# A graph network's first 112 nodes leave the count matrix and get their neighbours by row gathers

## The chip, the cores and the metric

The kernel runs on one core of one Trainium2 chip. The metric is the device time of one execution, in microseconds (us). The kernel before was run three times: 517.18, 517.28 and 517.34 us, median 517.28.

## The reference, cut to what matters

A graph has 2500 nodes with 256 numbers each and 80000 edges, sorted by target node. The input is normalized and clipped at zero, then three edge convolutions follow, and at the end a product with a wide matrix is added to the input:

```python
def _edge_conv(x, src, dst, W, b):
    m = concatenate([x[dst], x[src] - x[dst]], axis=-1) @ W + b      # W is 512 x 256
    s = segment_sum(m, dst, num_segments=2500)
    cnt = segment_sum(ones, dst, num_segments=2500)
    return s / maximum(cnt, 1.0)[:, None]

h = maximum(layernorm(x), 0.0); xs = [h]
for W, b in ((W0, b0), (W1, b1), (W2, b2)):
    h = relu(_edge_conv(h, src, dst, W, b)); xs.append(h)
return x + concatenate(xs, axis=-1) @ Wf + bf
```

A node's sum is its edge count times `h @ (W_top - W_bottom)`, plus the sum of the rows `z = h @ W_bottom` of the sources of its edges, plus the count times `b`.

## The kernel before, in words

**The count matrix.** The sum over sources is a dense matrix product. `A[s, n]` says how many edges run from node s to node n. The 2500 source nodes lie in NT = 20 tiles of 128, one tile after the other on the partitions. The target nodes are columns. Six neighbouring targets make a window (W = 6), 417 windows in all (NW). The windows are cut into five groups (GWS): four of 84 windows (504 columns) and one of 81 (486 columns). A group's part of A is a tile `a` of 128 x 20 x 512 floats (`new_a`, two of them in memory), of which 504 columns are used.

**Building A.** For each window the edges are fetched by an indirect transfer from GpSimd (`get_edges`, up to 256 edges for each of 128 windows). `compare` (lines 755 to 769) lets VectorE write one-hot matrices `one_m` and `one_n` for four windows at a time. `counts` multiplies them on TensorE into PSUM, two matmuls for each window. `take_counts` (line 782) lets ScalarE copy the result into `a`. `finish` (line 800) lets GpSimd put the edge counts themselves into a spare row of `a` (PAD = 96 of the last tile), so that `b` comes in by the same product, and stores the tile in HBM (`a_dram`), from where layers 2 and 3 load it (`load_a`).

**Aggregating.** `z` is held as two float32r halves, `zh` (rounded) and `zl` (the rest). `layer` (line 817) runs for each group 20 tiles x 2 column halves x 2 parts = 80 float32r matmuls of the group's width into `pa` (line 832), and then 4 float32 matmuls (8 records in the profile) that add `h @ (W_top - W_bottom)` times the count (line 836). ScalarE writes the clipped result into `hT` (line 839). `hT` holds h transposed: nodes in the columns.

**The order of the work.** Before line 847 comes a head: loading, normalizing, the first products, and the building of group 0. Its order is written out by hand as a string of short names (lines 864 to 873); the recorder `InOrder` (line 270) keeps program order on each engine, and what is recorded by it shows as line 280 in the profile. In layer 1 (`l = 0`, lines 900 to 928) the groups run from 0 to 4, and the building of the next group is spread between the matmuls of the present one. In layers 2 and 3 (`l = 1, 2`, lines 931 to 958) first `nodes_split` (line 708) computes z for all 20 tiles (2 matmuls each, line 711), which ScalarE and VectorE split into `zh` and `zl`. Then for each group come the `final` products of its tiles (line 734, with VectorE adding into `acc` at line 736) and `layer`. Layer 2 runs the groups backwards. In layer 2 `add_x` (line 724) loads each tile of x from GpSimd's queue and adds it and `bf`, on GpSimd. The last 20 `final` products and the stores of the output end the kernel.

The `bank` tiles of PSUM, which `nodes_split` and `final` share, are four in number here. In SP's queue stand the stores and loads of `a`, the weights and the output. In GpSimd's queue stand the indirect transfers and the loads of x.

Of the kernel before, what the change touches and what calls it, by code (L numbers as in the profile page):

```python
# [311 lines left out]
def by_windows(ctx: ExitStack, tc: tile.TileContext, x, src, dst, Ws, bs, Wf, bf, out, missing):  # L312
# [15 lines left out]
    CAP = CH * P  # L328
    NW = (N + W - 1) // W
    NV = NW * W  # L330
    WG = (NW + P - 1) // P
    NB = NT * W
    BW = 4
# [4 lines left out]
    while sum(GWS) < NW:  # L338
        GWS.append(min(84, NW - sum(GWS)))
    G = max(GWS) * W  # L340
    GS = 512
    NG = len(GWS)
# [6 lines left out]
    assert NP <= 4096 and HR <= 512  # L349
    assert E == P * R and NV <= NP and BW * NB <= 512 and G <= 512 and CAP <= 256  # L350
    assert E + P < 2 ** 24 and NV - (NT - 1) * P <= PAD < P and D == DC * P

# [35 lines left out]

    const.tile([P, 24], F32, name="between")
    a_dram = [dram.tile([P, NT, G], F32, name=f"a_dram{g}") for g in range(NG)]  # L390

# [42 lines left out]

    lim_i = pp.tile([P, WG], I32, name="lim_i")
    POOLo.iota(lim_i, pattern=[[P * W, WG]], base=0, channel_multiplier=W)
    limr_i = pp.tile([P, WG * P], I32, name="limr_i")
    POOLo.iota(limr_i, pattern=[[W, WG * P]], base=0, channel_multiplier=0)
    row_i = pp.tile([P, MORE], I32, name="row_i")
# [14 lines left out]
    DVE.memset(ones_b, 1.0)  # L454
    DVE.memset(cnt[:, NV:], 0.0)
    POOL.tensor_copy(ident_b, ident)
    warm = pp.tile([P, 1], F32, name="warm")
    ACTo.activation(warm, ones, AF.Sqrt)
# [95 lines left out]
    def key_parts(i):  # L554
# [4 lines left out]
        parts[i] = [lo_i]  # L559

    def key_low(i):
        km = pw.tile([P, CAP], F32, name="km")
        ACTo.copy(km, parts[i][0])
        parts[i][0] = km

    def key_high(i):

        hi_i = edges[i][0]
        DVEo.tensor_scalar(hi_i, hi_i, ~(P - 1), 4, op0=OP.bitwise_and, op1=OP.logical_shift_right)
        kn = pw.tile([P, CAP], F32, name="kn")  # L570
        DVEo.scalar_tensor_tensor(kn, away[:, i, :], float(W), hi_i, op0=OP.min, op1=OP.add)
        parts[i].append(kn)
# [15 lines left out]
    def degrees(i):  # L588

        for q in range(W + 2):  # L590
            junk = hot.tile([P, CAP], BF16, name="junk2")
            ACTo.activation(junk, away[:, i, :], AF.Relu, bias=nc_[:, q:q + 1], accum_out=gsum[:, i, q:q + 1])
            yield
        DVEo.scalar_tensor_tensor(deg[:, i, :], gsum[:, i, 1:W + 1], -2.0, gsum[:, i, 0:W], op0=OP.mult, op1=OP.add)
        DVEo.tensor_add(deg[:, i, :], deg[:, i, :], gsum[:, i, 2:W + 2])
        DVEo.tensor_copy(deg_b[:, i, :], deg[:, i, :])
        yield
        yield
        yield
        yield  # L600
        for w0 in range(0, min(P, NW - i * P), P // 2):
            n = min(P // 2, NW - i * P - w0)
            pc = bank()
            for c in range(W):
                PEo.matmul(pc[:, :n * W].rearrange("p (w c) -> p w c", c=W)[:, :, c],
                          deg_b[:, i, c:c + 1].to_broadcast([P, P]), ident_b[:, w0:w0 + n], start=True, stop=True)
            ACTo.copy(cnt[:, (i * P + w0) * W:(i * P + w0 + n) * W], pc[:, :n * W])
            yield

    def shares():  # L610
        cnt_n = bank()
        for t in range(NT):
            PEo.matmul(cnt_n[:, t:t + 1], cnt[0:1, t * P:(t + 1) * P], ones_b, start=True, stop=True)
        found = hot.tile([P, 1], F32, name="found")
        DVEo.reduce_sum(found, deg.rearrange("p i c -> p (i c)"), axis=mybir.AxisListType.X)
        pf = bank()
# [90 lines left out]

    def nodes_split(l, t):
        pz = bank()
        for c in range(DC):  # L710
            PE.matmul(pz[:, :D], hT[:, c, t * P:(t + 1) * P], ws[l][1][:, c, :],  # L711
                      start=(c == 0), stop=(c == DC - 1))
        sc = share[:, t:t + 1]
        if t == NT - 1:
            zf = hot.tile([P, D], F32, name="zf")
            DVE.scalar_tensor_tensor(zf, pz[:, :D], sc, brow[:, l % 2, :], op0=OP.mult, op1=OP.add)
            ACT.copy(zh[:, t, :], zf)
            DVE.tensor_sub(zl[:, t, :], zf, zh[:, t, :].bitcast(F32))
        else:
            ACT.activation(zh[:, t, :], pz[:, :D], AF.Copy, scale=sc)  # L720
            DVE.scalar_tensor_tensor(zl[:, t, :], pz[:, :D], sc, zh[:, t, :].bitcast(F32),  # L721
                                     op0=OP.mult, op1=OP.subtract)

    def add_x(t):
        n = P if t < NT - 1 else LAST
        xb = hot.tile([P, D], F32, name="zf")
        POOL.dma_start(xb[:n], x[t * P:t * P + n, :])
        POOL.tensor_add(xb[:n], xb[:n], bf_sb[:n])
        POOL.tensor_add(acc[:n, t, :], acc[:n, t, :], xb[:n])

    def final(l, t):
        po = bank()
        for c in range(DC):
            PE.matmul(po[:, :D], hT[:, c, t * P:(t + 1) * P], wfs[l][:, c, :],  # L734
                      start=(c == 0), stop=(c == DC - 1))
        DVE.scalar_tensor_tensor(acc[:, t, :], po[:, :D], share[:, t:t + 1], acc[:, t, :], op0=OP.mult, op1=OP.add)  # L736
        if l == L:
            n = P if t < NT - 1 else LAST
            SP.dma_start(out[t * P:t * P + n, :], acc[:n, t, :])


    def group_of(g):
        return sum(GWS[:g]) * W, GWS[g] * W

# [55 lines left out]
    def finish(g, a):  # L800
        c0, n = group_of(g)
        POOLo.tensor_copy(a[PAD:PAD + 1, NT - 1, :n], cnt[PAD:PAD + 1, c0:c0 + n])
        SP.dma_start(a_dram[g][:, :, :n], a[:, :, :n].bitcast(F32))
# [8 lines left out]
    def by_count(g):  # L812
        c0, n = group_of(g)
        for o in range(DC):
            DVEo.tensor_mul(hT[:, o, c0:c0 + n], hT[:, o, c0:c0 + n], cnt[:, c0:c0 + n])

    def layer(l, g, a, own, PE=PE, ACT=ACT):
# [29 lines left out]
    groups = [(0, 1), (1, 2), (2, 4), (4, 6), (6, 8), (8, Q)]  # L847
    a = new_a(0)
    acts = {
        "lim": limits, "first": find_first, "next": find_next, "pick": find_rows,  # L850
        "dstr": lambda: ACTo.copy(dst_r[:, MORE:], dst_i),
        "pk": lambda i: pick_half(i // 10, i % 10), "sg": lambda i: count_half(i // 10, i % 10),
        "se": lambda i: search(*((0, 1), (1, WG))[i]), "ge": get_edges,
        "ka": key_parts, "km": key_low, "kb": key_high, "kt": key_turn,
        "k1": lambda i: key_copy(i, 0), "k2": lambda i: key_copy(i, 1),
# [3 lines left out]
        "Z": lambda q: product(q, ws[0][1]), "V": lambda q: with_b(), "H": split_high, "L": split_low,  # L859
        "F": lambda q: product(q, wfs[0]), "G": first_final,  # L860
        "B": compare, "C": counts, "E": lambda b: take_counts(b, a),
        "warm": keep_warm,
# [6 lines left out]
        k11 N8 L6 B4 E2 L5 C3 B5 C4 T8 E3 E4 C5 V9 R8 E5 ge3 ka2 H9 sc2 Z7 H7 F8 G7 B6 N3 N2 ka3 km2 T2 R2 km3  # L869
        kb2 C6 T3 kb3 B7 L7 kt2 Z2 B8 B9 L9 E6 C7 k22 k12 kt3 H2 N4 E7 B10 k13 k23 Z8 L2 C8 T4 C9 E8 C10 H8 E9  # L870
        F9 B11 B12 C11 G8 E10 C12 R4 E12 E11 B13 F5 B14 C13 R3 B15 C14 E13 E14 L8 B16 Z3 G9 B17 C15 C16 H3 E15
        G5 B18 F3 C17 E16 C18 F4 E17 B19 C19 Z4 L3 G3 B20 E18 C20 B21 F2 E19 B22 E20 H4 L4 G4 B23 B24 G2 ws
    """
# [23 lines left out]
    held = None  # L897
    LATE = [NT] * 4
    extra = chain(degrees(0), finish(0, a), later_loads(), degrees(1))
    for g in range(NG):  # L900
# [12 lines left out]
        for u, _ in enumerate(layer(0, g, a, own, PEo, ACTo)):  # L913
# [7 lines left out]
            if u == NT - 1 and g + 1 < NG:  # L921
                run(extra)
                by_count(g + 1)
        run(extra)
        if g + 1 < NG:
            run(finish(g + 1, a1))
            held, a = a, a1
        extra = chain(degrees(g + 2) if g + 2 < WG else ())
    DVEo.tensor_sub(ws[1][0], ws[1][0], ws[1][1])
    tiles = {NG - 1: a, NG - 2: held}  # L930
    for l in range(1, L):
# [3 lines left out]

        last = touched(groups[0])
        for t in [t for t in range(NT) if t not in last] + last:
            nodes_split(l, t)
        if l + 1 < L:
            load_b(l + 1)  # L940
            load_wb(l + 1)
            load_wt(l + 1)
        finished = set()
        for j, g in enumerate(groups):
            for t in touched(g):
                if t not in finished:
                    finished.add(t)
                    final(l, t)
                    if l == 1:
                        add_x(t)  # L950
            if j == NG - 1:
                load_wf(l + 1)
            run(layer(l, g, tiles[g], LATE))
            if j == 1 and l + 1 < L:
                DVEo.tensor_sub(ws[l + 1][0], ws[l + 1][0], ws[l + 1][1])
            if j + 2 < NG:
                del tiles[g]
                tiles[groups[j + 2]] = load_a(groups[j + 2])

    for t in [*range(NT - 3), NT - 1, NT - 3, NT - 2]:  # L960
# [39 lines left out]
```

## Time and profile before

| | us |
|---|---|
| median of three runs | 517.28 |
| the profiled execution, whole | 517.24 |
| its span, first to last instruction | 515.4 |
| head, until the matmuls of group 0 begin | 62.33 |
| layer 1, groups 0 to 3 with the building of the next | 127.85 |
| layer 1, group 4 | 20.34 |
| `nodes_split` of layer 2, then its five groups | 17.27, then 124.25 |
| `nodes_split` of layer 3, then its five groups | 17.26, then 124.01 |
| last products and output | 22.09 |

The stages are cut where the chain of work that ended last passes from one to the next. The profile lists engines as PE (TensorE's matmuls), PEld (its weight loads, which run beside matmuls), DVE (VectorE), ACT (ScalarE), POOL (GpSimd) and SP (SyncE, which here issues transfers). A busy time is the time in which at least one instruction of the engine runs; matmuls are pipelined, so the duration of a record is longer than the distance from its start to that of the next, and only the distance counts in a sum. The chain follows the work back from the last instruction, at each step to what released it.

### The profile page before, as it was taken

Reading aid. Unit: us, or ns where it says so; the run is one execution under the profiler, and the core shown is the slowest. Engines: PE = TensorE matmul, PEld = TensorE weight load, DVE = VectorE, ACT = ScalarE, POOL = GpSimd, SP = SyncE. Lnnn points to the kernel's source line nnn. Section 1 sums busy time; section 2 is a strip of 40 time slices with the busy share of each in tenths; the row PEclk is TensorE's granted clock in tenths of the full one; section 3 lists DMA queues with packets and bytes.
Section 4 is the critical chain, followed back from the end, with each engine's and each line's share of the span. In section 5 each row is a group of like instructions: output and inputs, shape, how many; then the busy total and the mean of one; then the engine's idle time right before and its main releaser. Section 6 shows DMA issues by size and latency. Waiting matters only on the chain.

```text
span 515.4 us, 6981 instructions
## 1 busy us (share of the span) xinstructions
PE 508.1 (99%) x2864; PEld 407.2 (79%) x2864; DVE 213.5 (41%) x455; ACT 134.1 (26%) x307; POOL 68.5 (13%) x103
## 2 busy tenths in 40 slices
PE   8999999999999999999999999999999999999996
PEld 4898888778778788788787878787887878787875
DVE  7989998889888840360101010103501010101033
ACT  5776666644534320330000000004300000000000
POOL 2680000000000000017241424200000000000000
PEclk9999999999999999999999999999999999999999
DMA  9110008950906428011576665100005565730023
GB/s 277 50 43 0 1 2 325 336 215 15 378 11 232 171 80 318 22 31 48 180 261 207 236 229 214 32 1 1 1 0 197 205 219 183 252 136 20 1 84 121
DMA packets 38111, 68.74 MB, mean 133 GB/s; under 512 B 1201, under 2 KB 37065, under 8 KB 38071
## 3 DMA queue, kind: packets, MB, share of 16 engines
q1 hardware_dynamic: 35798, 63.49, 34.8%
q0 software_dynamic: 1344, 3.61, 2.3%
q10 hardware_dynamic: 928, 1.11, 0.7%
q8 instruction: 24, 0.39, 0.3%
q14 instruction: 17, 0.13, 0.1%
HBM read 40.03 MB, written 28.18 MB: 132 GB/s over the span
## 4 chain that ended last, share of the span: by engine, by line
PE 90%; DVE 4%; DMA 3%; POOL 2%; issue 1%; SPq 0%; DVEq 0%
PE pa L832 35%; PE pa L280 21%; PE bank L734 10%; PE bank L280 8%; PE bank L711 7%; PE pa L836 7%; PE pz L280 2%; DMA acc<-in_x_dram 2%; POOL acc L280 1%; DVE one_m L280 1%; DVE st L280 1%; DMA es<-in_src_dram,start_i 1%; POOL ed L280 1%; DVE one_n L280 1%; POOL es L280 0%
## 5 line engine op out<-in xcount | busy, mean ns | idle before, releaser
L832 PE MATMUL pa<-a,zh 128*128 128x504 f32 (+1 forms) x400 | 156.4, 391 | 0.0
L832 PE MATMUL pa<-a,zl 128*128 128x504 f32 (+1 forms) x400 | 154.5, 386 | 0.0
L736 DVE SCALAR_TENSOR_TENSOR acc<-bank,share,acc 128x256 f32<-128x256 f32 x60 | 29.0, 484 | 213.6 <-PE bank L734 213.5
L832 PEld LDWEIGHTS pa<-a,zh 128*128 128x128 f32 x400 | 75.2, 188 | 14.9
L832 PEld LDWEIGHTS pa<-a,zl 128*128 128x128 f32 x400 | 75.1, 188 | 14.8
L280 PE MATMUL pa<-a,zh 128*128 128x504 f32 (+1 forms) x200 | 84.0, 420 | 0.0
L280 DVE TENSOR_TENSOR one_m<-iota_m,key_m 128x1024 bf16<-128x1024 bf16 (+1 forms) x105 | 72.1, 687 | 15.2 <-PE bank L280 15.1
L280 PE MATMUL pa<-a,zl 128*128 128x504 f32 (+1 forms) x200 | 77.7, 389 | 0.0
L839 ACT ACTIVATE hT<-pa 128x1008 f32<-128x1008 f32 (+1 forms) x10 | 10.1, 1005 | 238.8 <-PE pa L836 238.8
L280 ACT CAST a<-bank 128x480 fp32r<-128x480 f32 (+1 forms) x105 | 52.9, 565 | 68.5 <-PE bank L280 65.9
L280 DVE TENSOR_TENSOR one_n<-iota_n,key_n 128x960 bf16<-128x960 bf16 (+1 forms) x105 | 69.7, 664 | 0.0
L734 PE MATMUL bank<-wf,hT 128*128 128x256 f32 x240 | 53.6, 379 | 0.0
L734 PEld LDWEIGHTS bank<-wf,hT 128*128 128x128 f32 x240 | 45.6, 190 | 9.8 <-issue 4.1
L280 PEld LDWEIGHTS <-one_m 128*128 128x128 bf16 x834 | 45.5, 98 | 9.8 <-issue 7.0
L280 PE MATMUL bank<-one_n,one_m 128*128 128x120 bf16 x834 | 51.4, 217 | 0.3
L280 PEld LDWEIGHTS pa<-a,zh 128*128 128x128 f32 x200 | 37.8, 189 | 10.3 <-issue 2.6
L280 PEld LDWEIGHTS pa<-a,zl 128*128 128x128 f32 x200 | 37.7, 189 | 8.9 <-issue 2.6
L721 DVE SCALAR_TENSOR_TENSOR zl<-bank,share,zh 128x256 fp32r<-128x256 f32 x38 | 18.4, 484 | 56.0 <-ACT zh L720 55.9
L836 PE MATMUL pa<-hT,wt 128*128 128x504 f32 (+1 forms) x80 | 35.2, 582 | 0.0
L711 PE MATMUL bank<-wb,hT 128*128 128x256 f32 x160 | 34.9, 379 | 0.0
L711 PEld LDWEIGHTS bank<-wb,hT 128*128 128x128 f32 x160 | 30.4, 190 | 4.9 <-issue 0.9
L836 PEld LDWEIGHTS pa<-hT,wt 128*128 128x128 f32 x80 | 15.1, 189 | 14.5 <-issue 13.8
(113 smaller groups left out, 333.2 us busy)
## 6 DMA issues: line engine op xcount, KB each, us to landing
a<-a_dram SPq DMA_DIRECT2D x5, 5040.0 KB, 17.3
a_dram<-a SPq DMA_DIRECT2D x4, 5040.0 KB, 17.2
a_dram<-a SPq DMA_DIRECT2D x1, 4860.0 KB, 17.1
a<-a_dram SPq DMA_DIRECT2D x1, 4860.0 KB, 15.1
zf<-in_x_dram POOLq DMA_DIRECT2D x19, 128.0 KB, 4.2
out_dram<-acc SPq DMA_DIRECT2D x19, 128.0 KB, 1.7
wf<-in_L_gnn_Wf_dram SPq DMA_DIRECT2D x4, 256.0 KB, 9.0
acc<-in_x_dram SPq DMA_DIRECT2D x1, 896.0 KB, 10.1
```

What stands on the lines that cost most here:

```text
L280: return self.tc.keep_in_program_order(call(*args, **kwargs))
L711: PE.matmul(pz[:, :D], hT[:, c, t * P:(t + 1) * P], ws[l][1][:, c, :], start=(c == 0), stop=(c == DC - 1))
L721: DVE.scalar_tensor_tensor(zl[:, t, :], pz[:, :D], sc, zh[:, t, :].bitcast(F32), op0=OP.mult, op1=OP.subtract)
L734: PE.matmul(po[:, :D], hT[:, c, t * P:(t + 1) * P], wfs[l][:, c, :], start=(c == 0), stop=(c == DC - 1))
L736: DVE.scalar_tensor_tensor(acc[:, t, :], po[:, :D], share[:, t:t + 1], acc[:, t, :], op0=OP.mult, op1=OP.add)
L832: PE.matmul(pa[:, o, :n], z[:, i, o * P:(o + 1) * P], a[:, i, :n], start=(i == 0 and z is zh), stop=(z is zl and last[o] == (kind, i, o)))
L836: PE.matmul(pa[:, o, :n], ws[l][0][:, c, o * P:(o + 1) * P], hT[:, c, c0:c0 + n], start=False, stop=(last[o] == (kind, i, o)))
L839: ACT.activation(hT[:, :, c0:c0 + n], pa[:, :, :n], AF.Relu)
```

## The change

The first FEW = 112 nodes are no longer columns of A. NW becomes 398 windows (2388 nodes), and the groups become four of 80 windows (480 columns) and one of 78 (468 columns); GS, the row length of `a`, becomes 480, so that four of the five tiles are stored and loaded as one run for each partition. `group_of` starts at column 112.

For the 112 nodes, `few_edges` (act `ix`) writes the numbers of up to EDGES = 60 sources of each into `who`, on the partitions 14 to 125 of the last batch of edges. Where there is no such edge it writes the last row, 2559, which is zero. z is kept in HBM as a table of rows, `z_dram[l]`:

- In layer 1, `keep_nodes` (acts `X` and `Y`) stores `zh` from SP and adds `zl` onto it from GpSimd, in five pieces. `gather(0)` then issues 60 indirect transfers from GpSimd, each of one row for every partition, that add into eight tiles `sums`; `add_sums(8)` lets VectorE add the eight.
- In layers 2 and 3 `nodes_split` writes z in float32 first (`zf`, on ScalarE, in memory of `one_m`, `sums` and `one_n`); SP stores it tile by tile, and VectorE makes `zh` and `zl` out of it with two instructions. `gather_pairs` issues 60 gathers, two for each of 30 pairs, into the four buffers of `one_m`, and VectorE adds each pair into `sums`, four pairs behind.
- `layer_few` runs at the end of each layer: for each column half 2 float32 matmuls with the weights, 2 float32r matmuls with `cnt_few` (for the count times `b`), and 1 float32 matmul with `only`, which places the gathered sums; all are 112 columns wide. ScalarE clips the result into the first 112 columns of `hT`.

`add_x` becomes `add_rest`: VectorE adds `bf` to a group's tiles at once, and GpSimd issues a transfer that adds x. The row of counts in `finish` is copied by ScalarE in place of GpSimd. The order string loses the windows 20 (C, E) and 24 (B) and gains `ix`, five `X` and five `Y`.

```diff
-    NW = (N + W - 1) // W
+    FEW = 112
+    EDGES = 60
+    SUMS = 8
+    PAIRS = 4
+    NW = (N - FEW) // W
...
-        GWS.append(min(84, NW - sum(GWS)))
+        GWS.append(min(80, NW - sum(GWS)))
     G = max(GWS) * W
-    GS = 512
+    GS = 480
...
+    def few_edges():
+
+        es, ed = edges[WG - 1]
+        own = pp.tile([P, EDGES], I32, name="own")
+        POOLo.tensor_scalar(who, es[:, :EDGES], -NONE, None, op0=OP.add)
+        POOLo.tensor_scalar(own, away[:, WG - 1, :EDGES], 0.0, None, op0=OP.is_equal)
+        POOLo.tensor_tensor(who, who, own, op=OP.mult)
+        POOLo.tensor_scalar(who, who, NONE, None, op0=OP.add)
...
-            ACT.activation(zh[:, t, :], pz[:, :D], AF.Copy, scale=sc)
-            DVE.scalar_tensor_tensor(zl[:, t, :], pz[:, :D], sc, zh[:, t, :].bitcast(F32),
-                                     op0=OP.mult, op1=OP.subtract)
...
+            ACT.activation(zf, pz[:, :D], AF.Copy, scale=sc)
+        SPo.dma_start(z_dram[l][t * P:(t + 1) * P, :], zf)
+        DVEo.tensor_copy(zh[:, t, :], zf)
+        DVEo.tensor_sub(zl[:, t, :], zf, zh[:, t, :].bitcast(F32))
...
+    def gather(l):
+
+        for e in range(EDGES):
+            POOLo.indirect_dma_start(
+                out=sums[:, e % SUMS, :], out_offset=None, in_=z_dram[l][:, :],
+                in_offset=bass.IndirectOffsetOnAxis(ap=who[:, e:e + 1], axis=0),
+                **({"compute_op": OP.add} if e >= SUMS else {}))
...
+    def gather_pairs(l):
+
+        got = []
+        for k in range(EDGES // 2 + PAIRS):
+            if k >= PAIRS:
+                if k == PAIRS + 1:
+                    DVEo.tensor_add(sums[:, :2, :], got[0], got[1])
+                elif k > PAIRS:
+                    DVEo.tensor_add(sums[:, :2, :], sums[:, :2, :], got[k - PAIRS])
+            if k < EDGES // 2:
+                two = room()
+                got.append(two)
+                for i in range(2):
+                    POOLo.indirect_dma_start(
+                        out=two[:, i, :], out_offset=None, in_=z_dram[l][:, :],
+                        in_offset=bass.IndirectOffsetOnAxis(ap=who[:, 2 * k + i:2 * k + i + 1], axis=0))
+            if k >= PAIRS - 1:
+                yield
+
+    def layer_few(l):
+        pa = ps_agg.tile([P, DC, 512], F32, name="pa")
+        for o in range(DC):
+            for c in range(DC):
+                PEo.matmul(pa[:, o, :FEW], ws[l][0][:, c, o * P:(o + 1) * P], hT[:, c, :FEW],
+                           start=(c == 0), stop=False)
+            for z in (zh, zl):
+                PEo.matmul(pa[:, o, :FEW], z[:, NT - 1, o * P:(o + 1) * P], cnt_few, start=False, stop=False)
+            PEo.matmul(pa[:, o, :FEW], sums[:, 0, o * P:(o + 1) * P], only, start=False, stop=True)
+        ACTo.activation(hT[:, :, :FEW], pa[:, :, :FEW], AF.Relu)
...
+    gather(0)
     extra = chain(degrees(0), finish(0, a), later_loads(), degrees(1))
...
+    add_sums(SUMS)
+    layer_few(0)
     DVEo.tensor_sub(ws[1][0], ws[1][0], ws[1][1])
...
+        last = [t for t in touched(groups[0]) if t]
+        for t, zf in zip([t for t in range(1, NT) if t not in last] + last + [0], rooms(l)):
+            nodes_split(l, t, zf)
+        few = gather_pairs(l)
+        next(few)
...
-            run(layer(l, g, tiles[g], LATE))
+            for u, _ in enumerate(layer(l, g, tiles[g], LATE)):
+                if 4 <= u < NT and u % 2 == 0:
+                    next(few, None)
+                if rest and u in (1, NT):
+                    next(rest, None)
...
+        run(few)
+        add_sums(2)
+        layer_few(l)
```

In the order in which the changed kernel is built, TensorE has 1200 float32r matmuls of aggregation as before (960 of 480 columns, 240 of 468), 796 count matmuls in place of 834, the same number of line 711 and 734 products, and 16 more records in each layer for `layer_few`, which stands behind the last group of its layer. In layers 2 and 3 tile 0, whose columns `layer_few` writes last, is the last that `nodes_split` treats. VectorE's 29 additions of pairs stand in its queue between the `final` additions of one group and those of the next: 7, 8, 8 and 6 of them.

## The prediction

> **What bounds the kernel now.** I read the busy times and the slices first, then the chain of waits by line and in order of time, then the stages, then the rows of the transfers that the change multiplies.
>
> ```profile
> PE 508.1 (99%) x2864; PEld 407.2 (79%) x2864; DVE 213.5 (41%) x455; ACT 134.1 (26%) x307; POOL 68.5 (13%) x103
> ...
> POOL 2680000000000000017241424200000000000000
> ...
> PE 90%; DVE 4%; DMA 3%; POOL 2%; issue 1%; SPq 0%; DVEq 0%
> PE pa L832 35%; PE pa L280 21%; PE bank L734 10%; PE bank L280 8%; PE bank L711 7%; PE pa L836 7%; PE pz L280 2%; DMA acc<-in_x_dram 2%; POOL acc L280 1%; DVE one_m L280 1%; DVE st L280 1%; DMA es<-in_src_dram,start_i 1%; POOL ed L280 1%; DVE one_n L280 1%; POOL es L280 0%
> ```
>
> A busy TensorE alone proves little; the chain does: 90% of it is TensorE, 56% the aggregation alone (L832 35%, L280 21%). POOL, which gets the new work, is empty for most of the span. The chain in order of time gives prices free of overlap:
>
> ```profile
> 78.93 1.28 PE bank L280 x24
> ...
> 210.52 17.27 PE bank L711 x80
> ...
> 256.41 18.15 PE pa L832 x80
> 274.56 3.38 PE pa L836 x8
> ...
> 472.70 17.34 PE pa L832 x80
> 490.05 3.26 PE pa L836 x8
> ```
>
> A 504-column matmul costs 18.15/80 = 226.9 ns, a 486-column one 17.34/80 = 216.8; a float32 record 422 and 407; a count matmul 1.28/24 = 53. In layer 1 VectorE might share the bound, so I read its stage (columns: stretch, its length, then busy us and count of PE, PEld, DVE, ACT, POOL; clock, DMA share, GB/s):
>
> ```profile
> 62.33:190.18 127.85, 127.85 (x1088) 101.04 (x1086) 106.89 (x189) 64.42 (x160) 4.37 (x6) 1.00 0.47 170
> ```
>
> VectorE has 21 us to spare there. TensorE's own work adds up to 320 x 227 + 666 x 53 + 32 x 422, some 122 us, and a few us of small products: this stage too is TensorE's.
>
> Last the gathers, as GpSimd issues them, and a comparison of VectorE beside one of them and beside none:
>
> ```profile
> 21.00 0.98 POOL L280 DMA_INDIRECT ed<-in_dst_dram,start_i  x1 [1.47 <-DVE start_i L280]
> 22.28 0.95 POOL L280 DMA_INDIRECT es<-in_src_dram,start_i  x1 [0.31 <-issue]
> ```
> ```profile
> 22.44 0.68 DVE L280 TENSOR_TENSOR one_m<-iota_m,key_m 128x1024 bf16<-128x1024 bf16 x1
> ```
> ```profile
> 38.61 0.68 DVE L280 TENSOR_TENSOR one_m<-iota_m,key_m 128x1024 bf16<-128x1024 bf16 x1
> ```
>
> One gather of 128 rows of 1 KB, the size of the new ones, takes GpSimd 1.28 us from start to start (1.48 at most). VectorE's comparison lasts 0.68 us beside it and 0.68 us alone.
>
> [...]
>
> **What the change removes, on the path.**
> - 960 matmuls go from 504 to 480 columns. The two measured widths give 10.1 ns for 18 columns, so 13.5 for 24; in proportion, 226.9 x 480/504 = 216.1, 10.8 ns less. But 486 columns took 17.60 us for 80 (220 ns) in the first group of layer 2, with other traffic about, so the slope may be as low as 6. I take 10.4: 10.0 us (bounds 5.8 and 13.0).
> - 240 matmuls go from 486 to 468: 8 ns each, 1.9 us.
> - 96 float32 records lose 24 columns (20 ns) and 24 lose 18 (15 ns): 2.3 us.
> - 38 count matmuls at 53 ns: 2.0 us.
>
> Sum 16.2 us. Five comparison windows less on VectorE, five PSUM copies less on ScalarE: nothing, off the path.
>
> **What it adds on the path.** `layer_few` has 12 float32 records and 4 float32r matmuls of 112 columns. The 128-column float32 transposes of the head follow each other at 109 ns in the timeline: 12 x 109 = 1.3 us; the others scale to 50 ns, I take 75: 0.3. So 1.6 us a layer, 4.8 in all (bounds 3.6 and 7.2[...]). At the end the last products start with tile 0, which needs the clipped `layer_few`: TensorE stops for ScalarE's pass of 224 columns (the 972-column one takes 0.98 us, so about 0.4) and two handovers: 0.65 us. After layers 1 and 2 `nodes_split` treats tile 0 last, 16 us later, so nothing. New handovers elsewhere: 0.5 us as an estimate. Sum 5.95 us.
>
> **What it adds beside the path.**
> - Head: `ix` and the `Y` transfers come after GpSimd's last normalizing, where POOL is free; SP's `X` stores stand ahead only of the store of group 0, which is issued some 15 us later. GpSimd's six more small set-up instructions fit in its 8 us of idling before the first fetch. Nothing.
> - Layer 1: 60 gathers x 1.28 = 77 us from about 70 us on, ready near 150. Needed near 198. Three additions on VectorE (about 2.3 us) wait for the last; behind them stand only weights for the next layer. Were the cover gone, TensorE would wait in front of `layer_few`.
> - `nodes_split`: VectorE now has two instructions a tile, about 0.7 us, against TensorE's 17.27/20 = 0.86. The first aggregation uses tile 0, done last, but five `final` products (4.3 us) lie between. SP issues 20 stores at 0.52 us each, ahead of the loads of `a`, which come 20 us later. Nothing.
> - Layers 2 and 3: the table is in HBM about 4 us after `nodes_split`; 60 gathers end at 4 + 77 + 3 = 84 us, in layer 2 some 9 us later for the six transfers of x. `layer_few` needs them after 20 products (17.3), five groups (86.2) and the weights (16): 119 us. An addition on VectorE that waits for a pair holds up the `final` additions behind it, but those free PSUM banks that TensorE wants one group (24 us) later. So nothing, with 26 to 35 us in hand.
> - Traffic: a load of `a` lands in 17.3 us and has 31 (it is issued when a group's matmuls end and needed one group and two rounds of `final` and weights later). A gather of 128 KB adds about 0.4 us of every DMA engine in 1.28, a third: 17.3 becomes some 23 us. Nothing, 8 us in hand. The accumulating transfers of layer 1 are not in this trace;[...] I take once.
> - The counts' row on ScalarE and `add_rest` are off the path, like what they replace.
>
> **Sum.** 515.4 - 16.2 + 5.95 = 505.15 us of span; 517.24 - 515.4 = 1.84 us lie around it, so 507.0 us. The profiled execution and the median of the runs differ by 0.04 us.
>
> **The rivals.**
> - *The gathers are too slow.* If a gather takes r us, they end in time for r up to (119 - 17)/60 = 1.7 in layer 2, (119 - 8)/60 = 1.85 in layer 3 and about 2.0 in layer 1. Beyond that TensorE stands in front of `layer_few`, 60 us for each us of r, in layer 2 first. The gain of 10.25 us is gone at r = 1.87. At r = 2.0 it waits 18 + 9 us: 534 us, slower. For it: a wait ahead of nearly every gather,[...] half of the rows being row 2559. Against: 1.28 to 1.48 us in the trace, beside busy engines, and four pairs in flight.
> - *Narrower matmuls pay less than their columns,* or waits of a few us arise at the new joints: at 5 ns in place of 10.4 the gain shrinks by 5 us, 512 us. For it: the 220 ns above. Against: 216.8 in layer 3.
> - *More is gained:* 13.5 ns and the low end of `layer_few`: 502.5 us.
>
> **How the numbers follow.** The forecast, 503 to 511 by the bounds of its terms, has 0.66; the rival of narrow matmuls and small waits 0.17 (510 to 517); the slow gathers 0.12; more gain 0.05. A measurement tells 0.2%, 1 us, from no change. Faster: 0.66 + 0.05 + 0.14; the same 0.03, the upper end of the second rival; slower 0.12. The range 502.5 to 514 leaves out the slow gathers and the tails, under 0.2.
>
> **What would show it.** Right: 80 matmuls of L947 in 17.2 to 17.4 us, records of 112 columns near 1.6 us a layer, no idle TensorE ahead of `only`, gathers 1.3 to 1.5 us apart. Wrong: TensorE waiting for DVE `sums`, or for the load of `a`; gathers 1.9 us apart; `bank` products waiting for VectorE.

## The result and the profile after

The changed kernel takes 553.97 us in the median of four runs (549.29 to 556.34), the kernel before 517.31 beside it: a ratio of 1.070, 95% interval 1.062 to 1.078. It is slower by 36.7 us; the prediction was 507.0. The profiled execution took 549.29 us, its span 547.6.

| stage, us | before | after | as predicted |
|---|---|---|---|
| head and layer 1, up to the first product of layer 2 | 210.5 | 206.0 | 205.4 |
| `nodes_split` of layer 2, its groups, `layer_few` | 141.5 | 152.9 | 138.4 |
| the same of layer 3 | 141.3 | 165.2 | 138.1 |
| last products and output | 22.1 | 23.5 | 23.2 |

Head and layer 1 gained nearly what was forecast (206.0 us against 205.4). All of the loss lies in layers 2 and 3, 14.5 and 27.1 us over the forecast. From the page of the changed kernel: busy times, slices, and the chain by engine.

```profile
PE 511.1 (93%) x2875; PEld 415.1 (76%) x2875; DVE 263.9 (48%) x556; ACT 136.3 (25%) x310; POOL 261.3 (48%) x243
...
PE   8999999999999999994999999999939999984996
...
POOL 4782278878788800277564534002762755400000
PEclk9999999999999999996899999999968999996999
...
PE 85%; DMA 9%; issue 4%; DVE 1%; ACT 0%; SPq 0%; DVEq 0%; ACTq 0%
```

TensorE was without a hole before; now there are three, in slices 19, 30 and 37, each with a lower granted clock (0.64 from 247.8 to 261.9 us, 0.64 from 397 to 414.6, 0.69 from 490.4 to 499.9). The chain in order of time shows what they are. Where it passes through the first one, in layer 2:

```profile
227.64 17.04 PE pa L947 x80
244.68 3.14 PE pa L951 x8
247.82 1.29 PE bank L781 x6
249.12 1.56 issue
250.68 0.38 PE bank L781
251.05 1.78 issue
252.83 0.59 PE bank L781
...
261.93 19.28 PE pa L947 x80
```

The 12 products of the second round of `final` (2.6 us of work) take 14 us, with gaps of 0.8 to 1.8 us between single records. "issue" says that the profile shows nothing that TensorE waited for, and no engine or transfer is named. So I looked at what the others did when it ended. ScalarE's clipping of the group whose last weight product ended at 247.8 (columns: start, length, engine, line, operation, idle time before):

```profile
262.19 0.95 ACT L954 ACTIVATE hT<-pa 128x936 f32<-128x936 f32 x1 [38.35 <-PE bank L781]
```

SyncE's load into the tile that the same group has read:

```profile
262.03 0.32 SPq L856 DMA_DIRECT2D a<-a_dram  x1
```

And GpSimd's gathers (the last of 24 in a row):

```profile
255.87 0.94 POOL L280 DMA_INDIRECT one_m<-z_dram,who  x1 [0.30 <-issue]
257.12 0.94 POOL L280 DMA_INDIRECT one_m<-z_dram,who  x1 [0.30 <-issue]
258.05 2.44 POOL L280 DMA_DIRECT2D acc<-in_x_dram  x2
```

ScalarE, SyncE and VectorE all begin at 262.0 to 262.2 with what TensorE had finished from 244.5 on: up to 17 us late, all at once, soon after the gathers stopped. In the kernel before this clipping followed the last record after 0.04 to 0.1 us. The trace also has, for each signal of an engine, the moment at which it was counted: for TensorE's up to 17.33 us after the end of the record that sends it, for those that it has of VectorE, ScalarE and GpSimd within 0.03 us. In what follows, a signal is late by that distance. So what came late was TensorE's signals, and from 249.1 us on TensorE itself crawled. Layer 3 has the same from 397 to 414.6, beside gathers that run from 379.3 to 409.3. There, signals were up to 6.7 us late beside a later row of 16 gathers, from 420.0 to 440.4; TensorE waited for none of them. For layer 2 a lack of instructions is unlikely: no packet of the two queues of kind `instruction` (q8 and q14 on the page) starts between 241.1 and 266.7, and the crawl ended between them, at 261.9.

The third hole is a load. The chain at its end:

```profile
460.44 39.30 DMA a<-a_dram
499.74 0.14 issue
499.87 19.28 PE pa L947 x80
```

The last load takes 39 us (15 to 17.5 before), TensorE waits 9.4 of them, and then runs 19.28 us at a clock of 0.88 in place of 17.05. The gathers' packets of 4096 bytes took 578 ns in the mean from 440 to 492 us, 218 from 379 to 410. Late gathers find few nodes with edges left, so nearly all of their rows are row 2559 (the fullest of the 112 nodes has 47 edges).

The gathers were not late. `layer_few` never waited, and in layers 2 and 3 they came every 1.25 us (1.28 predicted):

```profile
L280 POOL DMA_INDIRECT one_m<-z_dram,who x120 | 117.5, 979 | 150.0 <-DVE acc L280 65.4
...
L280 POOL DMA_INDIRECT sums<-z_dram,who x60 | 100.2, 1670 | 25.3 <-issue 17.1
```

### The profile page after: what moved, and what is told of

Read it like the earlier page. It is cut to its first block, busy times and chain, and to the rows that moved or that the text cites. A ratio compares the mean times of both kernels' runs of the same rounds, so it can differ in the third digit from the quotient of the medians.

```text
span 547.6 us, 7491 instructions
## 1 busy us (share of the span) xinstructions
PE 511.1 (93%) x2875; PEld 415.1 (76%) x2875; DVE 263.9 (48%) x556; ACT 136.3 (25%) x310; POOL 261.3 (48%) x243
## 4 chain that ended last, share of the span: by engine, by line
PE 85%; DMA 9%; issue 4%; DVE 1%; ACT 0%; SPq 0%; DVEq 0%; ACTq 0%
PE pa L947 29%; PE pa L280 20%; PE bank L781 9%; PE bank L280 9%; DMA a<-a_dram 7%; PE bank L757 6%; PE pz L280 6%; PE pa L951 5%; DMA wf<-in_L_gnn_Wf_dram 2%; PE turned L280 1%; DMA dst_i<-in_dst_dram 1%; DVE one_n L280 0%; DVE one_m L280 0%; ACT hT L280 0%; DVE acc L280 0%
## 5 line engine op out<-in xcount | busy, mean ns | idle before, releaser
L280 POOL DMA_INDIRECT one_m<-z_dram,who x120 | 117.5, 979 | 150.0 <-DVE acc L280 65.4
L947 PE MATMUL pa<-a,zh 128*128 128x480 f32 (+1 forms) x400 | 156.1, 390 | 11.8 <-DMA a<-a_dram 9.4
L947 PE MATMUL pa<-a,zl 128*128 128x480 f32 (+1 forms) x400 | 153.8, 385 | 0.4 <-issue 0.4
L280 POOL DMA_INDIRECT sums<-z_dram,who x60 | 100.2, 1670 | 25.3 <-issue 17.1
L280 DVE TENSOR_TENSOR sums<-sums,one_m 128x512 f32<-128x512 f32 x56 | 38.8, 692 | 123.0 <-DMA one_m<-z_dram,who 118.8
L947 PEld LDWEIGHTS pa<-a,zl 128*128 128x128 f32 x400 | 76.6, 192 | 13.2 <-issue 0.9
L280 PE MATMUL pa<-a,zh 128*128 128x480 f32 (+1 forms) x200 | 81.6, 408 | 0.0
L280 DVE TENSOR_TENSOR one_m<-iota_m,key_m 128x1024 bf16<-128x1024 bf16 x100 | 68.8, 688 | 17.5 <-PE bank L280 15.4
L954 ACT ACTIVATE hT<-pa 128x960 f32<-128x960 f32 (+1 forms) x10 | 9.7, 968 | 271.2 <-PE pa L951 205.5
L280 PE MATMUL pa<-a,zl 128*128 128x480 f32 (+1 forms) x200 | 75.8, 379 | 0.0
L280 ACT CAST a<-bank 128x480 fp32r<-128x480 f32 x100 | 51.4, 564 | 58.9 <-PE bank L280 53.9
L280 DVE TENSOR_TENSOR one_n<-iota_n,key_n 128x960 bf16<-128x960 bf16 x100 | 65.2, 652 | 0.0
L951 PE MATMUL pa<-hT,wt 128*128 128x480 f32 (+1 forms) x80 | 37.7, 605 | 6.8 <-issue 6.8
```

What stands on the lines that cost most here:

```text
L280: return self.tc.keep_in_program_order(call(*args, **kwargs))
L947: PE.matmul(pa[:, o, :n], z[:, i, o * P:(o + 1) * P], a[:, i, :n], start=(i == 0 and z is zh), stop=(z is zl and last[o] == (kind, i, o)))
L951: PE.matmul(pa[:, o, :n], ws[l][0][:, c, o * P:(o + 1) * P], hT[:, c, c0:c0 + n], start=False, stop=(last[o] == (kind, i, o)))
L954: ACT.activation(hT[:, :, c0:c0 + n], pa[:, :, :n], AF.Relu)
```

## The experiments

Three theories at first. A: GpSimd's unbroken stream of gathers holds TensorE up. B: the bytes, and the one row that so many read, clog the DMA engines. C: the long contiguous rows of `a` collide with the gathers.

### e1 to e4: which part of a gather does it

e1 leaves out the gathers and pair additions of layers 2 and 3:

```diff
-        few = gather_pairs(l)
-        next(few)
+        few = iter(())
+        POOLo.memset(sums[:, :2, :], 0.0)
```

> Leaves out the gathers and pair additions of layers 2 and 3 (the first 112 nodes get no neighbours there); the stores of the z tables and all else stay. Theory A (GpSimd's unbroken stream of gathers holds TensorE up), theory B (the rows they read, half of them row 2559, clog the DMA engines) and theory C (the 38,400-byte rows of the loads collide with the gathers) all say that TensorE's two slow stretches (about 14 and 17 us) and the 9 us of waiting for the last load vanish: layers 2 and 3 take about 119 to 121 us each for their five groups, and the whole 507 to 511 us. If it stays above 525 us, the loss comes from the new stores, from the stacking of queues or from the narrower matmuls, and not from the gathers.

514.7 us. The groups of layers 2 and 3 took 120.6 us each, and no wait is left in them. The time is above the forecast of 507 to 511 because layer 1, which kept its gathers, waited 2.7 us for `sums`. So the gathers are the loss. The stores and the order of the queues cost little: layers 2 and 3 took 140.6 and 139.7 us where 138.4 and 138.1 were predicted.

e2 drops the masking, so that `who` holds whatever edges the batch has: `POOLo.tensor_copy(who, es[:, :EDGES])`.

> Every gather reads the sources of whatever edges stand in the batch, so that no row is read more often than others (it adds rows that don't belong to the node). Same number of gathers, same bytes. Theory B: the late gathers' packets stay at about 160 to 230 ns instead of 500 to 780, the last load of a lands in 15 to 23 us instead of 39, and the two slow stretches shrink or vanish: 510 to 525 us. Theory A: the slow stretches stay at 14 and 17 us because the stream is as unbroken as before; only the last load may recover: about 538 us. Theory C: all stays, 545 to 555 us.

536.15 us: the wait for the last load is gone, both crawls stay (16.3 us of "issue" waits). B is right for the load and wrong for the crawls.

e3 puts plain transfers in the gathers' place, e4 gathers 64 bytes for each partition:

```diff
-                    POOLo.indirect_dma_start(
-                        out=two[:, i, :], out_offset=None, in_=z_dram[l][:, :],
-                        in_offset=bass.IndirectOffsetOnAxis(ap=who[:, 2 * k + i:2 * k + i + 1], axis=0))
+                    r = (2 * k + i) % (NT - 1) * P                          # e3
+                    POOLo.dma_start(two[:, i, :], z_dram[l][r:r + P, :])    # e3
```

> In layers 2 and 3 GpSimd issues 60 plain transfers of 128 rows of the table in place of the indirect gathers (other rows than the graph asks for): the same queue, the same bytes, no row read twice in a row, no indices. Theory A, if the issuing itself holds TensorE up: slow stretches stay, about 535 to 550 us. Theory A, if it is what GpSimd does for an indirect transfer: stretches gone, 507 to 515 us. Theory B: no clogging, 507 to 520 us.

> In layers 2 and 3 each gather fetches 64 bytes for each partition in place of 1024 (other data than the graph asks for; the pair additions are as narrow). As many gathers, issued as fast, one sixteenth of the bytes. Theory A: the slow stretches stay at 14 and 17 us, about 535 to 545 us, only the last load recovers. Theory B and every theory of bytes: 507 to 512 us.

e3: 513.45 us, no slow record. e4: 541.78 us with both crawls, though each gather moves a sixteenth of the bytes. In e4 the last weight product of the first group of layer 2 ended at 251.6; ScalarE's clipping:

```profile
265.76 0.95 ACT L954 ACTIVATE hT<-pa 128x936 f32<-128x936 f32 x1 [38.15 <-remote]
```

So it isn't the bytes. What is left is the issuing of indirect transfers, one behind the other.

### e5 to e8: length, spacing, kind, and the hot row

e5 issues 12 gathers in each group: `if 4 <= u < (8 if j == 0 else 16) and u % 2 == 0:` in place of `if 4 <= u < NT and u % 2 == 0:`.

> Only the places change at which the pairs are issued: 6 pairs, 12 gathers, in each group of layers 2 and 3 in place of up to 24 in one stretch. Theory A1 (an unbroken stretch of gathers longer than about 16 to 20 us holds TensorE up; e4 with a sixteenth of the bytes was still held up): the stretches last some 15 us, TensorE's slow stretches of 14 and 17 us are gone, and what stays is the last load of a (up to 13 us of waiting and lower clock): 518 to 530 us. Theory A2 (each gather costs TensorE a little, no matter how they lie): the loss is only spread out, 545 to 556 us.

534.84 us, outside of both. The crawls are gone and the clippings come 0.04 to 0.1 us after the last product. But TensorE waits 15.2 us in all for `sums`, once in each layer: 4.2 in layer 1, whose gathers are as before, and 11.0 in layers 2 and 3, where the last 12 gathers now fall into the last group and read row 2559 there. Theory A1 stood, as far as the crawls go; my number left out that the gathers end later.

e6 puts two memsets of 256 columns behind each gather of layers 2 and 3.

> Two small memsets on GpSimd after each gather of layers 2 and 3 put them about 1.9 us apart in place of 1.25, in stretches as long as before in number and longer in time. Layer 1 has 60 gathers 1.85 to 2.35 us apart without a slow stretch. Theory A3 (the rate decides): slow stretches gone, 518 to 530 us with the last load as it was, and perhaps a wait of some us ahead of the first 112 columns, since 60 x 1.9 plus 8 us is about the 119 us there are. Theory A1 (the length of the stretch decides): slow stretches stay or grow, 550 us or more.

543.57 us. No crawl either, and no late clipping, with the gathers 1.8 to 2.3 us apart. The time went elsewhere: TensorE waits 15.3 us for VectorE's additions into `acc`, which stand behind pair additions that wait for slow rows, and 6.8 for `sums`. The spacing helped here, and not because the stretches are short: layer 3 has 52 gathers in a row over 100 us. The slow landings of row 2559 widened some of the gaps, so the smallest spacing that helps isn't told here.

e7 is e3 with each copy cut into two of 512 bytes.

> As e3, with each plain copy cut into two of 512 bytes a partition, so that GpSimd issues them in unbroken stretches of about 48 x 0.53 = 25 us, as long as those of the gathers. Theory A1 in the form that any long stretch of issuing on GpSimd holds TensorE up: slow stretches of some 5 us or more in the second group of layers 2 and 3, 520 to 540 us. In the form that only indirect transfers do it: none, 512 to 517 us as e3.

514.25 us, no slow record, though GpSimd issued 40 and 43 transfers in unbroken stretches of 21 and 23 us. Of the two kinds only the indirect ones had slow records beside them (the changed kernel, e2 and e4).

e8 spreads the empty places over 32 zero rows and leaves the result as it is:

```diff
+        POOLo.iota(none, pattern=[[1, EDGES]], base=0, channel_multiplier=1)
+        DVEo.tensor_scalar(half, none, 16, None, op0=OP.bitwise_and)
+        DVEo.tensor_scalar(none, none, 31, None, op0=OP.bitwise_and)
+        POOLo.tensor_tensor(none, none, half, op=OP.add)
+        POOLo.tensor_scalar(none, none, N, None, op0=OP.add)
...
-        POOLo.tensor_scalar(who, who, NONE, None, op0=OP.add)
+        POOLo.tensor_tensor(who, who, none, op=OP.add)
```

> Where a node has no more edges, the gather reads one of 32 zero rows of the table in turn, and not always row 2559; the result is unchanged. Theory B, for the last load alone (e2 with random rows lost the 9 us wait and kept the slow stretches): the last load of a lands in 15 to 23 us, the two slow stretches stay, 533 to 541 us. If 32 rows are still too few, the load stays above 30 us and the time above 545.

537.52 us: TensorE no longer waits for the last load, and the late packets take 182 ns in place of 578. Both crawls stay (18.3 us of "issue"). The row that all empty places shared cost 11.8 us against the changed kernel's profiled 549.29; in the changed kernel's own trace the wait of 9.4 us and the slower matmuls after it (2.2) come to 11.6.

### e9 to e12: together, and whose signals are late

e9 takes e5's places, e8's rows and `EDGES = 48`; e10 the spread rows with 14 gathers at most in a stretch and all 60; e11 is e9 with `GS = 484`.

> Three edits together: the short stretches of e5, the spread empty rows of e8, and EDGES = 48 in place of 60 (the fullest of the first 112 nodes has 47 edges; a node with more would still go the general way). If the three causes found so far are all there are (stretches of gathers that hold TensorE up, the row that all empty places read, gathers of layer 1 that come too late), TensorE never waits: layer 1 as in the changed kernel, to 206 us, then 303 us as in e1, and 1.8 around it: 509 to 512 us. Above 515 a fourth cause is open.

> Spread rows and stretches of 7, 7, 7, 7 and 2 pairs, but all 60 gathers. No slow stretch of TensorE; layer 1's adding gathers still come 2 to 5 us too late, and the last pairs of layers 2 and 3 may come late by some us: 511 to 518 us. If stretches of 14 gathers (17.5 us) are already too long, slow records come back in groups 2 to 4 and it is 520 us or more.

> e9 with GS = 484 in place of 480: the rows of a are no longer contiguous, so its stores and loads go in pieces of 1,920 bytes and not of 38,400. Theory C (the long pieces hold the gathers and the loads up): faster than e9 by 1 us or more. If they cost nothing once the gathers are in place: within 0.5 us of e9, or slower if the short pieces take the DMA engines longer.

e9: 511.2 us (510.09 to 514.41), ratio 0.9887 (0.9864 to 0.991): 1.1% below the kernel before. e10: 513.27, ratio 0.9934 (0.9911 to 0.9958), and 18.2 us after the start of a dense stretch in layer 3 its first two slow records begin. With none in the 15 us stretches of e5 and e9, and the crawl 18 to 21 us after the start in the changed kernel, this brackets the length of a dense stretch at which TensorE itself slowed in these traces. e11: 512.38 us, ratio 0.9904 (0.9868 to 0.994), not told apart from e9. The long rows stand in e9 too, without a crawl, so theory C doesn't explain the loss; whether they cost a us or so is beyond these few runs.

e12 adds a marker to the changed kernel:

```diff
+                    DVEo.tensor_copy(mark[:, k - PAIRS:k - PAIRS + 1], sums[:, 0, :1])
+                    ACTo.copy(seen[:, k - PAIRS:k - PAIRS + 1], mark[:, k - PAIRS:k - PAIRS + 1])
```

> The changed kernel, with a marker: after each pair addition VectorE writes one number for each partition and ScalarE copies it, so that the trace shows when ScalarE hears of VectorE during the stretch of gathers. Only TensorE's signals are held back: the copies follow their markers within 0.3 us, while the clipping of the first group of layer 2 comes some 14 us after its last matmul, as in the changed kernel. All signals are held back: the copies come many us late too, as a bunch when the stretch ends. Whole time 545 to 562 us.

553.25 us. In the same stretch of gathers, VectorE and then ScalarE in the timeline:

```profile
248.50 0.15 DVE L280 COPY mark<-sums 128x1 f32<-128x1 f32 x1
...
250.95 0.15 DVE L280 COPY mark<-sums 128x1 f32<-128x1 f32 x1
262.54 0.88 DVE L280 SCALAR_TENSOR_TENSOR acc<-bank,share,acc 128x256 f32<-128x256 f32 x2 [11.45 <-remote]
```
```profile
248.69 0.19 ACT L280 COPY seen<-mark 128x1 f32<-128x1 f32 x1 [2.21 <-DVE sums L280]
251.13 0.19 ACT L280 COPY seen<-mark 128x1 f32<-128x1 f32 x1 [2.25 <-DVE sums L280]
262.54 0.95 ACT L958 ACTIVATE hT<-pa 128x936 f32<-128x936 f32 x1 [11.22 <-remote]
```

ScalarE hears of VectorE within 0.04 us (248.50 + 0.15 to 248.69), and of TensorE, whose last product ended at 248.2, after 14.3. Of the signals that this trace keeps of TensorE, VectorE, ScalarE and GpSimd, only TensorE's were late, by up to 17.3 us; the others came within 0.03.

### e13 to e17: density or length, and the rest

e13 adds an unused tile of 48 bytes to e9, e14 is e8 with one memset behind each gather (`POOLo.memset(pause, 0.0)`).

> e9 with an unused tile of 48 bytes behind the indices, so that the tiles of the count matrix lie where they lie in the changed kernel, 64 bytes higher than in e9. In e9 and e11 an aggregation matmul of 480 columns took 218.4 and 216.9 ns, in the changed kernel and in all kernels with its memory layout 219.6 to 219.8, with gathers or without. If the place decides: 219.7 ns again. If it is the smaller number of gathers in e9: 218.4 stays. The whole is then 1 to 1.5 us or 0 us slower than e9.

> The changed kernel with the spread empty rows of e8 and one small memset after each gather of layers 2 and 3 (e6 had two, and row 2559 in all empty places, whose slow landings broke the stretches up): gathers about 1.55 to 1.6 us apart, stretches as long as they come. If the rate decides and this is slow enough: no slow records, 511 to 516 us. If only the length of the stretch without a pause decides, and a memset is no pause: slow stretches of 10 us and more, over 530 us.

e13: 511.42 us in one run; 80 aggregation matmuls take 17.58 us again (219.7 ns) where e9's took 17.46, with the same gathers. So the 1.5 ns go with the place of the tile, 64 bytes apart, and not with the gathers. e14: 512.62 us. The clipping of the first group of layer 2 comes 0.1 us after the last product, and the crawls are gone, with stretches of up to 41 us. But this trace can't show that the memset did it, because the traces are of two kinds. In those of the changed kernel, of e1 to e12 and of e15, some of TensorE's signals are 0.5 to 0.9 us late already in the head, and 0.6 to 7.4 in layer 1. In those of the kernel before, of e13, e14, e16 and e17, no signal of TensorE is late by more than 0.02 us anywhere: not beside the gathers of layer 1 in e13 and e14, which have no pause, and not in the stretches of 12 dense gathers of e13 and e16. The first kind ran on the chips 2, 4, 8 and 9 and the second on 6 and 12, as far as the record names them; the kernel before took 517.0 to 517.5 us on all six. So a run of the second kind tells nothing about what a pause removes.

e15 is e14 with 48 edges; e16 is e9, and e17 is e15, with the memset after each gather of layer 1 as well.

> e14 with EDGES = 48, and the tiles of the count matrix 64 bytes lower again (as in e9): one memset after each gather, the places of the pairs as in the changed kernel, spread empty rows. If a pause of 0.2 us between the gathers is all that is needed, this is as fast as e9 without moving any pair: 508 to 512 us, TensorE without a slow record and the clipping 0.04 to 0.1 us after the last matmul of each group. If the shorter stretches of e9 were needed as well, slow records come back and it is above 515 us.

> e9 with one edit: a memset after each gather of layer 1 too, whose first eight (they write and don't add) come 1.25 us apart and are followed by more at 1.6 to 1.9. In e9's and e15's profiles group 0 of layer 1 took 34.2 and 37.4 us from its first matmul to its last weight product, and 30.9 in e13's, and in the long ones ScalarE and VectorE heard of TensorE's count matmuls up to 2.3 us late. If this is the same holding back of signals: group 0 takes 30.9 to 31.3 us, the runs lie closer together than e9's 510.1 to 514.4, median 508 to 510 us. If it is the traffic of the stores of that time: unchanged, 511 to 514 us.

> e15 with the same edit in layer 1. Same theory: e15's runs of 511 to 523 us come together at 508 to 512 us; if group 0's loss has another cause, they stay as they are. A wait for a pair in the last group of layer 2 (4.3 us in e15) may stay.

e15: 513.76 us (18 executions from 511.15 to 517.85, two of 520.85 and 522.62), ratio 0.9927. Its trace, of the execution of 522.62, is of the first kind: in layer 1, whose gathers have no pause, TensorE's signals are up to 7.4 us late. In layers 2 and 3, where the memset stands behind each gather, none is late by more than 0.02 us, over stretches of up to 30 us. The gathers in the timeline of e15, and the clipping of the first group of layer 2, whose last product ended at 253.88:

```profile
237.14 0.95 POOL L280 DMA_INDIRECT one_m<-z_dram,who  x1 [0.17 <-issue]
238.09 0.33 POOL L280 MEMSET pause<- 128x256 f32 x1
238.58 0.95 POOL L280 DMA_INDIRECT one_m<-z_dram,who  x1 [0.16 <-issue]
```
```profile
253.98 0.95 ACT L963 ACTIVATE hT<-pa 128x936 f32<-128x936 f32 x1 [24.04 <-PE pa L960]
```

Here a gather every 1.45 to 1.96 us in place of 1.25, with another instruction between, was enough. This and e6 carry the finding about the pause. Length counts as well, as long as the gathers are dense: in the traces of the first kind, layers 2 and 3, signals were late by up to 2.7 us with 12 gathers in a row (e5, e9, e11), 3.9 with 14 (e10), 5.1 to 6.9 with 16 and 17.3 with 24 (the changed kernel, e2, e8, e12). The stretches of e5 and e9 cost nothing because TensorE waited for none of these signals, and not because none was late.

The profiles of e9 and e15 lose their time in group 0 of layer 1, during the first, dense gathers. ScalarE in e9, at the copy of a bank whose last count matmul ended at 82.4 (the count matmuls stand in the trace in order, eight to a copy):

```profile
83.25 0.19 ACT L280 ACTIVATION_READ_ACCUMULATOR junk<-away,nc__97 128x1 f32 x1
86.76 0.56 ACT L280 CAST a<-bank 128x480 fp32r<-128x480 f32 x1 [3.32 <-remote]
```

It copies 4.4 us late, where in e13 and e16 the same copy comes after 0.04. It is the same lateness, larger than the 2.3 us that I had expected, and it comes early: in e10, e11 and e15 a signal is 1 us late already 1 us after the first gather. With the pauses in layer 1, e16 takes 509.82 us (509.75 to 510.14), ratio 0.9859 (0.9844 to 0.9874), group 0 takes 30.8 us (34.2 in e9), and its four runs lie within 0.4 us where e9's six span 4.3. That this is due to the pauses isn't shown: e16's trace is of the second kind, and e13, of that kind and without pauses, has as short a group 0 (30.9); less some 1.6 us for the place of its tile, an estimate from the 0.12 us in each group, its 511.42 would be e16's time. e17: 511.66 (510.58 to 513.49), ratio 0.9897; what it loses to e16 is a wait of some 2 us for a late pair in layer 2, as in e14. e16 has the lowest median on record, 7.4 us ahead of the kernel before. From its chain in layer 2, where the changed kernel crawled:

```profile
243.84 3.14 PE pa L960 x8
246.98 2.59 PE bank L789 x12
249.57 17.45 PE pa L956 x80
```

## Why the prediction was wrong, step by step

**The step that failed** is in "What it adds beside the path": for layers 2 and 3 it costed 120 gathers at "nothing, with 26 to 35 us in hand". Their rate was right (1.25 us against 1.28), and none came too late. What was wrong is that a free queue and enough time were taken for the whole cost. Beside indirect transfers issued back to back, every 1.25 us, TensorE's signals, which everybody else on the path waits for, came up to 17.33 us late, and TensorE crawled: 13.2 us in layer 2 (14.1 us for 2.6 us of products, and 19.28 in place of 17.57 for the matmuls after it, at a clock of 0.91) and some 15 in layer 3 (its 27.1 over the forecast less 11.8 for the load). The crawl stayed with a sixteenth of the bytes (e4, 541.78 us), was absent with plain transfers (e3 513.45, e7 514.25), and was gone in layers 2 and 3 where memsets put the gathers 1.45 to 2.3 us apart (e6, e15). The two gathers in a row that I priced from could not show it. I bounded the gathers' duration, which the trace of before shows only in part, and not what a long row of them does to the other engines.

**Traffic** ("17.3 becomes some 23 us. Nothing, 8 us in hand") failed for one load of six: 39.3 us. I priced every gather's packets alike. That half of the rows were row 2559 stood in a rival, as a reason for late gathers; its real victim was the last load, 11.8 us with the clock (e8).

**Layer 1's gathers** "taken at once" a plain gather: they came 1.85 to 2.35 us apart, the last was issued at 190 and its sum needed at 204. The value was taken too low: they come some 1.4 to 1.8 times as far apart as the 1.28 us of a plain gather. It was just hidden in the changed kernel; e1, e3 and e4 waited 2 to 3 us for it, e5 4.2.

**VectorE's additions** that wait for a pair were to hold up only banks wanted a group later: true in the changed kernel, false as soon as the gathers come slower (15.3 us in e6).

**The sum on the path was nearly right.** Without the gathers' effects, e16 has a span of 508.1 us against 505.15: the start of layer 2 at 205.25 (205.4 predicted), layers 2 and 3 0.8 and 1.05 us longer, the end 1.25. Terms: 218 to 219.7 ns for a 480-column matmul, where 216.5 was taken; `layer_few` 1.77 us, not 1.6; and the last stores ended 5.9 us after the last addition in e16, 4.3 before. e16 computes 48 places in place of 60, which lie off the path.

**The rivals.** The slow gathers had the right sign and the wrong mechanism: their condition, r above 1.87 us, was never met in layers 2 and 3. Small waits and narrow matmuls (512) would have been the nearest to e9 to e16.

**What stays open.** Why TensorE's signals were late beside the indirect issuing isn't shown, nor why TensorE's records start some multiple of 0.7 us apart in the crawls (0.73, 1.41, 2.09 and 2.80 in layer 3 of the changed kernel); nor whether the memset helps by the 0.2 us or by being another kind of instruction. The largest open end is the two kinds of traces: no run on the chips 6 and 12 has stretches of 24 gathers without a pause, so whether the changed kernel would be slow there isn't known, and e14's success stays without a counterpart. The traces with late signals also lack records: of the marks of landed transfers e9's has 2783 and e13's, the same program but for 48 bytes, 4066. Whether the recording itself takes part isn't told by these runs. Spread rows were tried with 32 rows, not with fewer.

## What to carry to other kernels

An idle queue isn't a free one: before a step with many instructions of a kind goes "beside the path", ask what a dense row of them does to the engine on the path, and if the trace has no such row, keep both signs open. Before a cure is believed, look in the same trace for the trouble where the cure was not applied: e15 still has late signals in layer 1, so that their absence in layers 2 and 3 means something; e14 has none anywhere, so that it means nothing. When a profile shows gaps put down to "issue", look at what all other engines start at the moment the gaps end: here it named the late signals in three lines. Where indirect gathers stand in a long row, a short instruction between them is a cheap thing to try (it cost GpSimd 0.2 us for each gather), and so is spreading the rows that padding reads.

## What the runs showed of the hardware

- Indirect gathers 1.25 us apart, in the traces of the first kind (the changed kernel, e1 to e12, e15): TensorE's signals late by up to 2.7 us in stretches of 12 gathers and 17.3 in stretches of 24, and from 18 to 21 us on TensorE crawling with single records 0.7 to 2.8 us apart. In the same kind of trace, at 1.45 to 1.96 us apart with a memset between (e15): signals within 0.02 us, over 30 us.
- In e13 and e16, on the chips 6 and 12, 12 gathers in a row 1.25 to 2.2 us apart: signals within 0.02 us.
- Plain transfers from the same queue every 0.53 us for 23 us (e7): no such effect in layers 2 and 3. In the midst of the dense gathers (e12), VectorE's signal to ScalarE: 0.04 us.
- Gathers that nearly all read one row of 1 KB (the changed kernel, 440 to 492 us): 578 ns for each packet of 4096 bytes; spread over 32 rows (e8) 182.
- Accumulating gathers came 1.85 to 2.35 us apart, plain ones 1.25 (the changed kernel).
- A 480-column float32r matmul took 219.7 ns in e13 and 218.2 in e9, whose tiles of `a` lie 64 bytes apart. Such records last 0.38 us and start 0.22 us apart (e9, 83.32 and 83.54 us).
